# Four 64x64 products that stood in 128-row pairs are put beside the four mixing products, in one section of the step

## The chip, the cores and the metric

The kernel runs on one core of a Trainium2 chip. The metric is the device time of one execution in microseconds; of the kernel before there are three runs, and their median counts. A profile of one further execution is at hand.

## The reference

The input `x` is 16 images of 64 channels and 128 x 128 pixels in float32. Four residual layers follow one another, each on a group norm (32 groups of two channels) of its input:

```
x = x + L0(gn(x))   # gram = xf xf^T / N;  conv_w @ (gram @ xf): a 64x64 mixing of the channels of each image
x = x + L1(gn(x))   # |scharr_x| + |scharr_y|, each channel by itself
x = x + L2(gn(x))   # a quarter of the channels shifted left, a quarter right; 3x3 conv 64->64; bias
x = x + L3(gn(x))   # 3x3 conv 64->64, 1x1 conv 64->64, batch norm over all images, leaky relu, clip to 0..255
```

Layer 3's batch norm needs sums over all images, so the kernel keeps its result in memory and ends with a pass that reads it and layer 3's input back, combines them and writes the output.

## The kernel before, in words

**Tiling.** The 128 partitions hold two halves of 64 channels. For layer 0 and 1 these are the upper and the lower half of an image, eight rows of each at a time (`R = 8`, so an image has `NS = 8` pieces). Layers 2 and 3 hold even and odd rows ("planes"); a piece makes two output tiles of four row pairs.

**Steps and stages.** One loop goes over steps; a step has four quarters, q = 0 to 3. In every quarter the stages run in the order `Layer3`, `Layer2`, `Front` (layers 0 and 1), each on the piece of the image that is due, and then the `Gram` part for a later image. Each image is eight steps behind the one before it, so in a middle step all stages are at work on different images. `InOrder` keeps every engine's instructions in the order in which the program issues them, so each engine is a fixed list; what an instruction waits for on other engines comes from the tiles it touches.

**What TensorE does in a step.** Each layer of 2 and 3 needs per step the shared products (`shared`, into the tile `one`: six products) and two sets of own products (`own`, n = 0 and n = 1, into the two banks of the tile `two`). All of these have 128 rows and 64 columns: the output is the lower 64 partitions or the upper 64, and `issue` alternates them, so that two run side by side in the two column halves of the array. I call two such products side by side a pair slot. `own` works on a difference tile (`diffs`, `d` in the profile: odd rows minus even rows and the like). In one output half both input planes have weights: three products, one for each tap kx. In the other half (`o` from `single`) only one input plane has weights: two of its taps are packed into one product of 128 rows (weights `pk`, source `qd`, a copy of the difference whose second half is shifted by a column), and the last tap, kx = 2, is a product of 128 rows of whose weights 64 rows are zero:

```
some[o] = [
    (p[cols(o), 0:m], pk, q[:, :, 1:1 + W]),
    (p[cols(o), 0:m, 0:W - 1], wt[:, n, 2, cols(o)], d[:, :, 2:1 + W]),
]
```

I call this product the sparse last tap. There are two in each layer and step (n = 0, 1), four in a step.

**The mixing.** For image 3 and later (`four`), the layer-0 product of a piece is four products of 64 rows and 64 columns, in quarter 1 (`mix_four`). `load` puts the first four rows of both image halves into partitions 0 to 63 and the second four into 64 to 127. So the two products of g = 0 use the upper row half of the array and write both column halves of the tile `po`, and those of g = 1 the lower row half and a tile of the pool `ps_g` (`po` too in the profile). The steps with this mixing are 104: 13 images by 8. In them layers 2 and 3 are always at work.

**The order around the change.**
- Quarter 0: VectorE drains layer 2's `two` of the step before (`two<-two,edges`, then `x<-two,c`) and makes layer 2's difference n = 0 (`difference("d2", 0, ...)`); a DMA on GpSimd's queue makes its shifted copy (`twin(0)`, `qd<-d`). TensorE does layer 3's `shared` and `own` n = 0.
- Quarter 1: layer 3's `own` n = 1; `issue_rest` sends what is held back; then `mix_four`; then, in three of eight steps while there are images left, 42 to 44 Gram products (`bank<-xw`).
- Quarter 2: layer 2's `shared`, its tile `two` is taken from the pool (`ps_two`, two buffers, which layers 2 and 3 take in turn), `own` n = 1. ScalarE empties `one` (`c<-one,co`). VectorE drains layer 3's `two` (`y<-two,c`) and makes layer 3's differences (`d3`).
- Quarter 3: layer 2's `own` n = 0, and after it VectorE's difference n = 1 for the next step ("last of 3").

VectorE also does layer 1 (the tiles `u` and `e`), ScalarE the norms, absolute values and sums of squares (`junk`). When an image's layer 2 is through, VectorE reduces its sums (`s<-st`) and makes the next image's weights (`wi`).

Of the kernel before, what the change touches and what calls it, by code (L numbers as in the profile page):

```python
# [16 lines left out]
P = 128  # L17
# [3 lines left out]
R = 8  # L21
# [88 lines left out]
def tile_kernel(ctx: ExitStack, tc: tile.TileContext, x, cw_h, w2_t, b2, wbin_t, w1_t, b1, gamma, beta, consts, out):  # L110
# [56 lines left out]
    def cols(o):  # L167
        return slice(o * C, (o + 1) * C)
# [372 lines left out]
    class Front:  # L541
# [14 lines left out]
        def load(self, i):  # L556
            b = self.b
            t = xin.tile([P, R, W], F32, tag="x", name=f"x_{b}_{i}")
            if self.four:

                t = t.rearrange("p (h r) w -> p h r w", h=2)
                v = x[b].rearrange("c (h r) w -> c h (r w)", h=2)
                for g in range(2):
                    j = (i * R + g * CP) * W
                    sp.dma_start(t[cols(g)].rearrange("p h r w -> p h (r w)"), v[:, :, j:j + CP * W])
            else:
                for h in range(2):
                    sp.dma_start(flat(t[h * C:(h + 1) * C]), halves(x[b].rearrange("c h w -> (c h w)"), h, i * R, R))
            self.xs[i] = t

        def mix_four(self, i):

            for g, (pool, tag) in enumerate(((ps_po, "po"), (ps_g, "g"))):
                self.po[i, g] = pool.tile([P, CP, W], F32, tag=tag, name=f"po_{self.b}_{i}_{g}")
            t = self.xs.pop(i)
            order = 1 - last[0], last[0]
            for g in range(2):
                for h in order:
                    pe.matmul(self.po[i, g][cols(h)], self.abd[cols(g), cols(g)], t[cols(g), h], start=True, stop=True)

        def mix(self, i, g):
            if self.b == 0 and (i, g) in ((0, 1), (1, 0)):
# [15 lines left out]
        def at(self, i, q):  # L598
            b = self.b
            if q == 0:  # L600
                if i == -3:

                    self.xe = xin.tile([P, W], F32, tag="xe", name=f"xe_{b}", bufs=1)
                    sp.dma_start(self.xe[lo], x[b][:, HH, :])
                    sp.dma_start(self.xe[hi], x[b][:, HH - 1, :])
                    sp.dma_start(x2_d[b][0:W].rearrange("(p w) -> p w", p=1), w0[0:1, 0:W])
                if i + 3 < NS and i + 3 not in self.xs:
                    self.load(i + 3)
                if -1 <= i < NS - 1:
                    self.prepare(i + 1, 1)  # L610
                if 1 <= i:
                    self.store(i - 1)
                    act.activation(
                        junk.rearrange("p (j w) -> p j w", w=W), self.x2.pop(i - 1), AF.Square,
                        accum_out=self.st[:, 1, i - 1:i],
                    )
                if i == NS:
                    chains.append(coefficients(self.st, lambda co: coefs2.update({b: co}), b2_sb))
            if q == 1 and -2 <= i < NS - 2:
                if i == -2:  # L620
                    self.abd, self.co = lead.pop(b)
                if i == -2 and not self.four:
                    self.pe = ps_g.tile([P, CP, W], F32, tag="g", name=f"pe_{b}")[:, 0, :]
                    small_product(self.pe, self.abd, self.xe)
                if self.four:
                    self.mix_four(i + 2)
                else:
                    self.mix(i + 2, 0)
            if q == 3 and i == -2 and self.four:
                self.pe = ps_po.tile([P, CP, W], F32, tag="po", name=f"pe_{b}")[:, 0, :]  # L630
                small_product(self.pe, self.abd, self.xe)
            if (i, q) == ((-1, 0) if self.four else (-2, 2)):
                nc.gpsimd.memset(self.chunk(0)[lo, 0, :], 0.0)
                self.normalized(self.chunk(0)[hi, 0, 1:1 + W], self.pe[hi], hi)
                self.pel = small.tile([P, W], F32, tag="pel", name=f"pel_{b}", bufs=1)
                self.normalized(self.pel[lo], self.pe[lo], lo)
            if q == 2:
                if i == NS - 2:
                    nc.gpsimd.memset(self.chunk(NS - 1)[hi, R + 1, :], 0.0)
                    act.copy(self.chunk(NS - 1)[lo, R + 1, 1:1 + W], self.pel[lo])  # L640
            if 0 <= i < NS:
                self.sobel(i, q)
            if q == 2 and -2 <= i < NS - 2:
                self.prepare(i + 2, 0)
            if q == 3 and -2 <= i < NS - 2 and not self.four:
                self.mix(i + 2, 1)
                self.xs.pop(i + 2)
# [71 lines left out]
        pe.matmul(dst, wt, src, start=start, stop=stop)  # L719
        last[0] = o  # L720

    def issue(halves):


        for o in range(2):
            for n, (dst, wt, src) in enumerate(halves[o]):
                held[o].append((dst, wt, src, n == 0, n + 1 == len(halves[o])))
        while held[0] and held[1]:
            o = 1 - last[0]
            emit(o)  # L730
            emit(1 - o)
# [10 lines left out]
    def shared(p, wt, t, m=CP):  # L742
        products(p[:, 0:m], [wt], [by_parity(t)[1][:, 0:m]])

    def own(p, n, table, wt, name, m=CP, both=None):
        d, q, pk = diffs[name][:, n, 0:m], twins[name][:, n, 0:m], packed[f"pk{name[1]}"][:, n]
        o, _ = single(table, n)
        some = [None, None]
        some[1 - o] = taps(1 - o, p[:, 0:m], [wt[:, n] if both is None else both], [d], 1)
        some[o] = [  # L750
            (p[cols(o), 0:m], pk, q[:, :, 1:1 + W]),
            (p[cols(o), 0:m, 0:W - 1], wt[:, n, 2, cols(o)], d[:, :, 2:1 + W]),
        ]
        issue(some)


    tiles3 = {}

    class Layer2:
# [65 lines left out]
        def at(self, i, q):  # L825
# [22 lines left out]
            if q == 1:  # L848
                if i == 0:

                    self.wi = stp.tile([P, 2, 3, P], F32, tag="wi", name=f"wi_{b}", bufs=1)
                    for n, base in ((0, w2[:, 2]), (1, wm)):
                        dve.scalar_tensor_tensor(
                            self.wi[:, n].rearrange("p k o -> p (k o)"), k("I3"), self.co[:, 2:3],
                            base.rearrange("p k o -> p (k o)"), op0=ALU.mult, op1=ALU.add,
                        )
                if -1 <= i < NS - 1:
                    if i == -1:
                        self.co = coefs2.pop(b)
                    t, f = self.v[i + 1], self.whole.pop(i + 1)  # L860
                    act.activation(f, f, AF.Identity, bias=self.co[:, 1:2], scale=self.co[:, 0:1])


                    e = stp.tile([P, 2, R], F32, tag="edges", name=f"edges_{b}_{i + 1}", bufs=3)
                    for side, at in ((0, 0), (1, W + 1)):
                        for rows, j in ((lo, 1), (hi, 0)):
                            n = at + j * W
                            pool.tensor_scalar_mul(
                                e[rows, side], f[rows, n:n + (R - 1) * W + 1:W], self.co[rows, 3 + side:4 + side]
                            )  # L870
                    self.edges[i + 1] = e

                    pool.tensor_scalar_mul(t[:, :, 0], t[:, :, 0], k("keep0"))
                    pool.tensor_scalar_mul(t[:, :, W - 1], t[:, :, W - 1], k("keep1"))
                if i + 2 < NS:
                    self.load(i + 2)
            if q == 2:
                if 0 <= i < NS:
                    t = self.v[i]
                    one = ps_one.tile([P, CP, W], F32, tag="one", name=f"one2_{b}_{i}")  # L880
                    two = ps_two.tile([P, 2, CP, W], F32, tag="two", name=f"two2_{b}_{i}")
                    self.p[i] = two, one
                    shared(one, self.wi[:, 0], t, m)
                    if closing:
                        small_product(one[:, m, :], w0, t[:, R, :])

                    both = self.wi[:, 1]
                    own(two[:, 1], 1, TO_SLOTS, w2, "d2", m, both)
                    if closing:

                        p = two[:, 1, m:CP]
# [8 lines left out]
            if q == 3:  # L900
                if 0 <= i < NS:
                    t = self.v.pop(i)
                    two, one = self.p[i]
                    both = self.wi[:, 1]
                    own(two[:, 0], 0, TO_SLOTS, w2, "d2", m, both)
                    if closing:
                        p, srcs = two[:, 0, m:CP], [t[:, R - 2:R - 1, :], t[:, R - 1:R, :]]
                        issue([taps(0, p, [w2[:, 0], both], srcs), taps(1, p, [both, w2[:, 1]], srcs)])
# [7 lines left out]
    class Layer3:  # L916
# [34 lines left out]
        def at(self, i, q):  # L951
# [10 lines left out]
            if q == 1:  # L962
                if 0 <= i < NS:
                    two, one = self.p[i]
                    own(two[:, 1], 1, TO_PAIRS, w3, "d3")
                    self.v.pop(i)
                    self.c = ring.tile([P, CP * W], F32, tag="c3", name=f"c3_{b}_{i}", bufs=1)
                    act.activation(self.c, flat(one), AF.Identity, bias=b1_sb)
# [82 lines left out]
    for step in range(starts[2][1] - 2, steps):  # L1051
        now[0] = step
        for q in range(4):
# [5 lines left out]
            for stage, at in starts:  # L1059
                if stage is Front and q in (1, 3):  # L1060
                    issue_rest()
                for b in range(B):
                    run(stage, b, step - at - NS * b, q)
            if q in (0, 3):
                for b in range(B):
                    run(Layer2, b, step - starts[1][1] - NS * b, f"last of {q}")
# [116 lines left out]
```

## Time and profile before

| | |
|---|---|
| median of 3 runs | 2716.55 us (2714.24 to 2718.3) |
| the profiled execution | 2713.5 us, of which 2711.7 us are its span |
| PE (TensorE matmul) busy | 2146.4 us (79%) |
| DVE (VectorE) busy | 2116.7 us (78%) |
| ACT (ScalarE) busy | 2069.4 us (76%) |
| POOL (GpSimd) busy | 1042.6 us (38%) |
| stretch with HBM at 420 GB/s, at the end | from about 2230 us to 2711.7 us |

Busy shares are averages over the whole span, so they mix three stages: the start, the steps, and the last pass. The mixing of 64-row products runs from 357.5 us on; the profile starts the steps that are looked at here at each `po<-x,abd 64*64`. In the trace each float32 product is two matmul records of half the time, so that a set of four products counts x8. The column "idle before" names what ended the idle time; "issue" is a wait that the profile can't name.

### The profile page before, as it was taken

How to read it: one execution, taken by the hardware profiler on the slowest of the kernel's cores; microseconds unless marked ns; L12 is line 12 of the kernel's file. 1: busy time of each engine (PE TensorE's matmuls, PEld its weight loads, DVE VectorE, ACT ScalarE, POOL GpSimd, SP SyncE). 2: the span in 40 equal slices, each digit the busy share in tenths (PEclk: the TensorE clock that was granted, in tenths of full speed). 3: DMA queues.
4: the chain of work that ended last, by engine and by line, in shares of the span. 5: the costliest groups of instructions: out<-in, count | busy, mean ns of one | idle time of the engine just before them, and what ended most of it. 6: DMA issues, size and time to landing. Idle time of an engine off the chain costs nothing. (4 is left out here: it accounts for less than half of the span.)

```text
span 2711.7 us, 45518 instructions
## 1 busy us (share of the span) xinstructions
PE 2146.4 (79%) x14804; PEld 905.4 (33%) x14804; DVE 2116.7 (78%) x3111; ACT 2069.4 (76%) x3001; POOL 1042.6 (38%) x1558
## 2 busy tenths in 40 slices
PE   6578899999999999999999999999999992000000
PEld 4234433434343434343434343333335641000000
DVE  4998899898989898989898999999994335333332
ACT  4766889898989898989899989999996666333332
POOL 2266545444445454444445454655554300000000
PEclk8689999999999999999999999999999996555555
DMA  8799889998999889898989888888887879999999
GB/s 208 204 236 241 223 197 245 225 237 222 236 225 241 227 230 230 227 231 232 229 228 237 214 216 204 212 216 218 220 204 187 219 197 327 420 420 420 420 420 374
DMA packets 693596, 685.92 MB, mean 253 GB/s; under 512 B 60096, under 2 KB 580448, under 8 KB 693360
## 3 DMA queue, kind: packets, MB, share of 16 engines
q1 hardware_dynamic: 668208, 613.83, 79.0%
q0 software_dynamic: 25152, 69.18, 10.0%
q8 instruction: 119, 1.95, 0.3%
q14 instruction: 117, 0.96, 0.1%
HBM read 346.23 MB, written 268.44 MB: 227 GB/s over the span
## 5 line engine op out<-in xcount | busy, mean ns | idle before, releaser
L73 PE MATMUL two<-d,w 128*64 128x508 f32 (+2 forms) x2560 | 835.7, 586 | 0.0
L73 PE MATMUL two<-d,wi 128*64 128x508 f32 (+3 forms) x1536 | 571.7, 576 | 0.0
L73 PE MATMUL two<-qd,pk 128*64 128x512 f32 (+1 forms) x1024 | 517.4, 586 | 25.7 <-DMA qd<-d 25.3
L73 POOL DMA_DIRECT2D qd<-d x512 | 272.3, 534 | 686.5 <-DVE d L73 277.9
L73 POOL TENSOR_SCALAR edges<-v,co 64x8 f32<-64x8 f32 x512 | 328.7, 642 | 274.7 <-ACT v L73 195.1
L73 DVE TENSOR_TENSOR d<-v 128x512 f32<-128x512 f32 (+1 forms) x512 | 346.7, 680 | 86.0 <-issue 50.4
L73 PEld LDWEIGHTS two<-d,w 128*64 128x64 f32 x2560 | 272.4, 136 | 322.8 <-issue 282.7
L73 PE MATMUL one<-v,w 128*64 128x508 f32 (+2 forms) x1600 | 364.4, 579 | 1.1 <-ACT v L73 1.1
L73 PE MATMUL one<-v,wi 128*64 128x508 f32 (+3 forms) x1536 | 355.8, 595 | 0.4 <-DVE wi L73 0.3
L73 ACT COPY qd<-d 64x512 f32<-64x512 f32 x512 | 315.6, 616 | 23.3 <-DVE d L73 13.8
L73 DVE SCALAR_TENSOR_TENSOR e<-e 128x1032 f32<-128x1032 f32 (+1 forms) x256 | 313.3, 1224 | 0.0
L73 ACT ACTIVATE xh<-po,co 128x128 f32<-128x128 f32 (+1 forms) x480 | 275.5, 624 | 28.9 <-PE po L73 25.0
L73 PEld LDWEIGHTS two<-d,wi 128*64 128x64 f32 x1536 | 178.6, 135 | 201.3 <-issue 183.2
L73 POOL TENSOR_SCALAR v<-v,kc 128x9 f32<-128x9 f32 x256 | 229.9, 912 | 12.0
L73 DVE SCALAR_TENSOR_TENSOR y<-two,c 128x1024 f32<-128x1024 f32 x128 | 156.0, 1219 | 98.0 <-ACT v L73 45.5
L73 PE MATMUL po<-x,abd 64*64 64x512 f32 (+1 forms) x1024 | 176.6, 639 | 43.9 <-ACT xh L73 38.2
L73 ACT ACTIVATE v<-x,co 128x1024 f32<-128x1024 f32 (+3 forms) x256 | 203.9, 847 | 0.0
L73 ACT ACTIVATE u<-u 128x1024 f32<-128x1024 f32 x128 | 135.6, 1060 | 81.6 <-DVE u L73 80.1
L73 ACT ACTIVATE c<-one,co 128x512 f32<-128x512 f32 x128 | 87.0, 679 | 140.2 <-PE one L73 140.1
L73 PEld LDWEIGHTS two<-qd,pk 128*64 128x64 f32 x1024 | 135.2, 136 | 164.6 <-issue 104.8
L73 PEld LDWEIGHTS one<-v,w 128*64 128x64 f32 x1600 | 130.5, 136 | 175.9 <-issue 147.3
L73 DVE SCALAR_TENSOR_TENSOR u<-xh 128x1170 f32<-128x1170 f32 x128 | 175.5, 1371 | 5.6 <-ACT xh L73 4.5
(160 smaller groups left out, 3432.1 us busy)
## 6 DMA issues: line engine op xcount, KB each, us to landing
x<-in_x SPq DMA_DIRECT2D x256, 256.0 KB, 4.7
x_d<-u SPq DMA_DIRECT2D x512, 128.0 KB, 4.1
y_d<-y SPq DMA_DIRECT2D x512, 128.0 KB, 3.5
x_d<-x SPq DMA_DIRECT2D x496, 128.0 KB, 3.1
xr<-in_x SPq DMA_DIRECT2D x120, 512.0 KB, 6.0
qd<-d POOLq DMA_DIRECT2D x256, 130.0 KB, 3.2
qd<-d POOLq DMA_DIRECT2D x256, 129.8 KB, 3.8
v<-x_d SPq DMA_DIRECT2D x448, 72.1 KB, 2.8
```

Of the source, the lines that this page charges most:

```text
L73: return self.tc.keep_in_program_order(call(*args, **kwargs))
```

## The change

The last taps leave `own` in all steps with mixing. They become products of 64 rows and 64 columns (only the plane that has weights), and go beside the mixing products:

- Layer 3's are noted at q = 1 after its `own` n = 1, and close their sums. Layer 2's are noted at q = 1 too, before its other products of q = 2 and q = 3, and open their sums (`start`); the tile `two` of layer 2 is taken at q = 1 for it.
- `mix_four` is now called for g = 0 and g = 1 and notes its two products each. `load` puts the two image halves into the two partition halves, as for the first three images, so a DMA's runs are 4 KB long where they were 2 KB. The two products of one g then use different row halves and different column halves of the array, and write one bank in different partitions.
- At the end of the quarter `issue_beside` sends layer 3's two taps, the two products of g = 0, layer 2's two taps, and the two products of g = 1.
- Steps without mixing issue what they issued.

On the other four engines the lists of instructions and their waits are the same, but for the shape of those loads. On TensorE the number of products stays the same.

```diff
         def load(self, i):
...
-            if self.four:
-                t = t.rearrange("p (h r) w -> p h r w", h=2)
-                v = x[b].rearrange("c (h r) w -> c h (r w)", h=2)
-                for g in range(2):
-                    j = (i * R + g * CP) * W
-                    sp.dma_start(t[cols(g)].rearrange("p h r w -> p h (r w)"), v[:, :, j:j + CP * W])
-            else:
-                for h in range(2):
-                    sp.dma_start(flat(t[h * C:(h + 1) * C]), halves(x[b].rearrange("c h w -> (c h w)"), h, i * R, R))
+            for h in range(2):
+                sp.dma_start(flat(t[h * C:(h + 1) * C]), halves(x[b].rearrange("c h w -> (c h w)"), h, i * R, R))
...
-        def mix_four(self, i):
-            for g, (pool, tag) in enumerate(((ps_po, "po"), (ps_g, "g"))):
-                self.po[i, g] = pool.tile([P, CP, W], F32, tag=tag, name=f"po_{self.b}_{i}_{g}")
-            t = self.xs.pop(i)
-            order = 1 - last[0], last[0]
-            for g in range(2):
-                for h in order:
-                    pe.matmul(self.po[i, g][cols(h)], self.abd[cols(g), cols(g)], t[cols(g), h], start=True, stop=True)
+        def mix_four(self, i, g):
+            pool, tag = ((ps_po, "po"), (ps_g, "g"))[g]
+            po = pool.tile([P, CP, W], F32, tag=tag, name=f"po_{self.b}_{i}_{g}")
+            t = self.xs[i][:, g * CP:(g + 1) * CP, :]
+            for h in range(2):
+                beside.append((po[cols(h)], self.abd[cols(h), cols(h)], t[cols(h)], True, True))
+            self.po[i, g] = po
...
+    def mixing():
+        i = now[0] - starts[2][1] - NS * EARLY
+        return -2 <= i < NS * (B - EARLY) - 2
+
+    def issue_beside():
+        for n in range(0, len(beside), 2):
+            for dst, wt, src, start, stop in sparse[n:n + 2] + beside[n:n + 2]:
+                pe.matmul(dst, wt, src, start=start, stop=stop)
...
     def own(p, n, table, wt, name, m=CP, both=None, apart=None):
...
+        some[o] = [(p[cols(o), 0:m], pk, q[:, :, 1:1 + W])]
+        if not mixing():
+            some[o].append((p[cols(o), 0:m, 0:W - 1], wt[:, n, 2, cols(o)], d[:, :, 2:1 + W]))
+            issue(some)
+        else:
+            issue(some, *((o, None) if apart == "before" else (None, o)))
+
+    def last_taps(two, table, wt, name, m=CP, first=False):
+        if mixing():
+            for n in range(2):
+                o, i = single(table, n)
+                sparse.append((
+                    two[cols(o), n, 0:m], wt[cols(i), n, 2, cols(o)], diffs[name][cols(i), n, 0:m, 2:2 + W],
+                    first, not first,
+                ))
...
# Layer2.at, q == 1
+                if 0 <= i < NS:
+                    self.two = ps_two.tile([P, 2, CP, W], F32, tag="two", name=f"two2_{b}_{i}")
+                    last_taps(self.two, TO_SLOTS, w2, "d2", m, True)
# Layer2.at, q == 2 and q == 3
-                    own(two[:, 1], 1, TO_SLOTS, w2, "d2", m, both)
+                    own(two[:, 1], 1, TO_SLOTS, w2, "d2", m, both, "before")
# Layer3.at, q == 1
                     own(two[:, 1], 1, TO_PAIRS, w3, "d3")
+                    last_taps(two, TO_PAIRS, w3, "d3")
# the loop over the quarters, after the stages
+            issue_beside()
```

More of the change, by code (lines that the diff above doesn't have):

```diff
@@ L625, in at @@
                 if self.four:
-                    self.mix_four(i + 2)
+                    for g in range(2):
+                        self.mix_four(i + 2, g)
+                    self.xs.pop(i + 2)
                 else:
@@ L720, in emit, with issue @@
         last[0] = o
-    def issue(halves):
+    sparse, beside = [], []
+    def mixing():
[5 more added lines that the diff above has]
+                pe.matmul(dst, wt, src, start=start, stop=stop)
+        for dst, wt, src, start, stop in sparse[len(beside):]:
+            pe.matmul(dst, wt, src, start=start, stop=stop)
+        last[0] = 1
+        sparse.clear()
+        beside.clear()
+    def issue(halves, before=None, after=None):
         for o in range(2):
             for n, (dst, wt, src) in enumerate(halves[o]):
-                held[o].append((dst, wt, src, n == 0, n + 1 == len(halves[o])))
+                held[o].append((dst, wt, src, n == 0 and before != o, n + 1 == len(halves[o]) and after != o))
         while held[0] and held[1]:
@@ L743, in shared, with own @@
         products(p[:, 0:m], [wt], [by_parity(t)[1][:, 0:m]])
-    def own(p, n, table, wt, name, m=CP, both=None):
+    def own(p, n, table, wt, name, m=CP, both=None, apart=None):
         d, q, pk = diffs[name][:, n, 0:m], twins[name][:, n, 0:m], packed[f"pk{name[1]}"][:, n]
@@ L749, in own @@
         some[1 - o] = taps(1 - o, p[:, 0:m], [wt[:, n] if both is None else both], [d], 1)
[L750 to L754, printed above, removed]
+        some[o] = [(p[cols(o), 0:m], pk, q[:, :, 1:1 + W])]
[12 more added lines that the diff above has]
+                ))
     tiles3 = {}
@@ L880, in at @@
                     one = ps_one.tile([P, CP, W], F32, tag="one", name=f"one2_{b}_{i}")
-                    two = ps_two.tile([P, 2, CP, W], F32, tag="two", name=f"two2_{b}_{i}")
+                    two = self.two
                     self.p[i] = two, one
@@ L904, in at @@
                     both = self.wi[:, 1]
-                    own(two[:, 0], 0, TO_SLOTS, w2, "d2", m, both)
+                    own(two[:, 0], 0, TO_SLOTS, w2, "d2", m, both, "before")
                     if closing:
```

## The prediction

> **What bounds the kernel now.** I read the page's 40 slices first, for the stages.
>
> ```profile
> PE   6578899999999999999999999999999992000000
> DVE  4998899898989898989898999999994335333332
> ACT  4766889898989898989899989999996666333332
> ```
>
> A slice is 67.8 us. PE is full from slice 6 to 33, but DVE and ACT stand at 8 to 9 until slice 30 (2006 us): three engines share this stage. Then PE alone is full, to about 2200 us, and the rest is the last pass, where the chain of waits is DMA out, x3 and y in turn. So I cut the stage at each mixing product and took every engine's busy time by windows, one step each. One image is eight steps:
>
> ```profile
> core 0: us, PE busy (x) PEld busy (x) DVE busy (x) ACT busy (x) POOL busy (x), PEclk, DMA share, GB/s
> 1267.79:1285.82 18.03, 18.03 (x170) 8.15 (x168) 17.77 (x30) 15.85 (x26) 7.90 (x13) 1.00 0.90 222
> 1285.82:1303.79 17.97, 17.97 (x174) 7.92 (x172) 16.26 (x27) 14.34 (x22) 5.63 (x10) 1.00 0.73 179
> 1303.79:1321.62 17.83, 17.83 (x170) 7.58 (x168) 15.44 (x28) 13.40 (x22) 11.49 (x18) 1.00 0.99 253
> 1321.62:1337.21 15.59, 15.59 (x115) 9.29 (x113) 11.42 (x19) 15.46 (x24) 7.52 (x12) 1.00 1.00 260
> 1337.21:1352.17 14.96, 14.96 (x77) 4.80 (x76) 14.85 (x24) 13.95 (x22) 8.02 (x10) 1.00 0.95 237
> 1352.17:1368.68 16.51, 15.07 (x74) 5.08 (x73) 16.48 (x22) 16.19 (x26) 8.24 (x12) 1.00 0.93 261
> ...
> sum 130.83, PE 129.39 PEld 52.41 DVE 121.80 ACT 118.95 POOL 62.17; mean PE 16.17 PEld 6.55 DVE 15.22 ACT 14.87 POOL 7.77
> ```
>
> The reader is to see that PE's 129.39 of 130.83 us hides a change of bound. In the first three steps PE also does Gram products and DVE has air. In the fourth ACT has none (15.46 of 15.59). From the fifth on DVE has none, and in the sixth PE itself idles 1.44 us. The timelines of the engines give the joints:
>
> ```profile
> 1295.06 0.69 DVE L73 TENSOR_TENSOR d<-v 128x512 f32<-128x512 f32 x1 [1.52 <-issue]
> 1310.53 0.69 ACT L73 ACTIVATE c<-one,co 128x512 f32<-128x512 f32 x1 [4.33 <-PE one L73]
> 1337.05 0.17 DVE L73 TENSOR_REDUCE s<-st 128x2 f32<-128x16 f32 x1 [3.43 <-ACT junk L73]
> ```
>
> DVE waits at 1295.06 until PE has read the difference it overwrites; ACT waits at 1310.53 for PE's `one`; then ACT runs gapless to 1337 and DVE waits for it; then DVE runs with no gap over 0.25 us to its first wait on PE at 1276.99 in the picture of one image earlier, that is 1407.8. So an image's 130.8 us are a ring: DVE 70.8, PE 33.5 (1276.99 to 1310.53), ACT 26.5. **Only what PE saves in its third of the ring counts.**
>
> **What the Trainium skill says.** "TensorEngine Tiling (Array Packing)", Key Properties: tiles run independently, and a change of tiling mode drains the array. The trace agrees, with its prices:
>
> ```profile
> 1302.84 1.02 PE L73 MATMUL two<-d,w 128*64 128x508 f32 x4
> 1303.79 1.09 PE L73 MATMUL po<-x,abd 64*64 64x512 f32 x8
> 1304.81 0.28 PE L73 MATMUL bank<-xw 128*64 128x65 f32 x2
> ```
>
> The four mixing products (x8) take 1.02 us to the next start. A pair slot takes 0.853 us (`two<-d,wi` at 1355.82 to the same place of the next tap at 1356.68 is 0.86). Four tiles thus cost one pair slot plus 0.16 of drain. The same page, Gotcha 1, says that different row tiles can't use the same PSUM bank at once; "PSUM — Partial Sum Buffer", PSUM bank collisions raise a hardware error, narrows this to one bank and 32-partition quadrant. The trace of before doesn't show the case: there the two row halves write different banks. After, the two products of a g write one bank from different row halves, in different quadrants. The second page would let them overlap, and so do I; the first is a rival below.
>
> **The change part by part.**
>
> *TensorE, per step.* Removed: four sparse taps, that is two pair slots, 2 x 0.853 = 1.71 us. Mixing grows from one set of four to two: 1.02 becomes 2 x 0.853 + 0.16 = 1.87. Net 0.853 us a step, 88.7 us over 104 steps. That is work, not time. The new section is unseen: bounds 1.87 (all overlap) and 3.57 (nothing across row halves, 4 x 0.853 + 0.16); I take 1.87. No cheaper end is to be had: 16 records in four tiles are 1.71 alone.
>
> *The new wait.* Layer 2's taps stand in the middle of the section and need `x<-two,c` done (the bank is free) and the difference n = 0, DVE's next instruction. Before, PE needed this difference only in quarter 3. Behind the wait on PE stand the products of g = 1, Gram, and `one`, and for these ACT. In the PE third the price is nil: the difference is done at 1282.0 and 1300.1, the sections start at 1285.82 and 1303.79, over 3.6 us later, and layer 2's taps come 0.85 us into them. In the DVE stretch PE arrives early and will wait here; DVE doesn't care: `one` follows 0.85 + 2.6 us after the difference and ACT's `c` in a light step comes about 5.7 after it. That the shifted copy is needed later in PE's list (one pair slot less before it, one set more) leaves the wait `two<-qd,pk` (1.44 us at 1359.99) off the path too.
>
> *Layer 3's sum* closes in the first set, 1.02 us after the section's start instead of 0.17. `y<-two,c` came 1.6 us after that start or later (1287.43 against 1285.82), and PE's lead covers the rest: nothing. The POOL and SP queues keep order and waits. The loads' 4 KB runs move the same bytes; PE waited for `x` once, 5.7 us: nothing.
>
> *What an image gains.* (a) Head start: at the section of 1267.79 the difference is there at 1266.5. PE, 0.85 us faster in each of the steps before, can be in the section's second half then, so start at 1265.7, 2.1 earlier; the section is 0.85 longer: 1.25 net. (b) Two further full steps to `one` at 1310.53: 2 x 0.853 = 1.71. Together 2.96 us; DVE's own waits on PE in this third (0.20 + 1.52 + 2.25 = 3.97) leave room for it. Then ACT, and so DVE's `s`, come 2.96 earlier. Late next is DVE, everywhere else in the ring.
>
> *Sum.* Nine such images (sections from 480 to 1613 us): 9 x 2.96 = 26.6. The steps from 357 to 480: DVE waits 1.84 us at one `s`, with ACT waiting more than that on PE before it: 1.8. The 26 steps after 1613 without Gram products: DVE is busy 205.16 of 210.10 us in the last 14; what PE can give back there are the waits at two `s` (1.18 and 1.96, ACT having waited for `one` before both): 3.1. At the end PE leaves the mixing 0.85 us ahead of the difference instead of 2.57 behind (1900.72 against 1898.15), and to 2200 us PE alone bounds: 3.4. The last pass is DMA's and only starts earlier. Total **34.9 us**. The profiled execution took 2713.5 (span 2711.7 and 1.8 around it), so 2678.6; it lies 3.05 below the median of 2716.55, so **2682** against that.
>
> **The rivals.**
>
> *PE is the bound in each step*, as its full row of nines says: the whole 88.7 us come, 2628. For it: PE has no gaps. Against: DVE's 14.85 of 14.96 and 16.48 of 16.51. A part of it (PE's lead carried over image borders) would give 2640 to 2660.
>
> *Slower: row halves that share a bank don't overlap.* The section costs up to 3.57. The point from which it decides is 1.02 + 1.71 = 2.73 us; above it PE gets slower than before, and PE has only 1.44 us of air per image. At 3.57 a step gains 0.85: an image's PE work becomes 129.4 + 6.8 = 136.2, 5.4 over now, nine times 49; of the other 33 or so steps nearly all are PE-full, 0.75 each, 25: 2790. For it: the page's sentence, and that no such set is in the trace. Against: pairs of `two<-d` share a bank from two column halves and overlap fully.
>
> *Nothing shows.* The ring's ACT and DVE parts stretch by what PE gives (ACT is within 0.13 us of full in the fourth step, and one `xh<-po` a little later would do): within 5 us of 2716.
>
> **How the numbers follow.** Central case 0.66 (2660 to 2708), whole or larger gain 0.10, nothing 0.06, slower 0.18 (most of it the shared bank, the rest a wait in the section that I priced at nil). A measurement of this kernel tells about 0.2%, 5.4 us, from no change. Faster 0.76, same 0.06, slower 0.18. The range 2640 to 2722 leaves out some 0.05 below and 0.13 above. The likeliest case's own range is 2660 to 2708.
>
> **What would show it.** In the profile after: `two<-d,w 64*64` and `po<-x,abd 64*64` in one section of 1.8 to 1.9 us where PE doesn't wait; DVE idle per image down from 9.0 to about 6 us; steps in the DVE stretch as long as now (14.4 to 16.5) with PE idle showing up in them; ACT's 4.33 us before `c<-one` about halved; the Gram steps 17.1 to 17.3 us instead of 18; the last pass as long as before. Wrong: sections of 2.7 us or more; or steps of 14.0 us in the DVE stretch (then DVE was not the bound); or DVE waits on `two` that were not there.

## The result, and the profile after

The kernel after took 2684.64 us (median of 4 runs, 2683.2 to 2690.18), the kernel before 2716.45 us (4 runs, 2714.24 to 2718.3). The ratio is 0.9887 with a 95% interval of 0.987 to 0.9904: 31.8 us faster, where 34.9 were worked out. The profiled execution of after is the slowest of its four, 2690.18 us with a span of 2688.4; against before's profiled 2713.5 it shows only 23.3 us, and the stages below add up to that number.

The page's slices of the kernel after:

```profile
PE   6578899999999999999999999999999992000000
DVE  4999899899999899999999999999994325333332
ACT  4766889898989898989899989999986676333332
```

PE's row of nines is what it was, although PE does less (a nine stands for anything from 90% up). The windows between the starts of the mixing sections, the same image as before (span; then busy time and instructions of PE, PEld, DVE, ACT, POOL; granted clock, DMA share, GB/s):

```profile
1254.61:1271.81 17.20, 17.20 (x172) 7.63 (x170) 17.10 (x31) 15.84 (x26) 8.57 (x14) 1.00 0.90 224
1271.81:1288.94 17.13, 17.13 (x176) 7.62 (x174) 16.69 (x28) 14.46 (x24) 6.04 (x10) 1.00 0.77 189
1288.94:1305.90 16.96, 16.96 (x172) 7.42 (x170) 15.45 (x28) 13.41 (x20) 9.88 (x17) 1.00 1.05 255
1305.90:1321.28 15.38, 15.38 (x117) 8.01 (x115) 13.04 (x18) 15.28 (x24) 8.49 (x12) 1.00 0.99 258
1321.28:1337.27 15.99, 14.80 (x80) 4.83 (x79) 14.13 (x22) 14.95 (x25) 8.64 (x12) 1.00 0.91 240
1337.27:1353.72 16.45, 14.45 (x76) 4.71 (x75) 16.38 (x23) 16.18 (x25) 7.89 (x11) 1.00 0.94 247
```

The three Gram steps lost 0.83 to 0.87 us each. The three steps after them together take 47.82 us where they took 47.06, and PE now idles in two of them (15.99 against 14.80, 16.45 against 14.45). One of the new sections, from PE's timeline:

```profile
1271.81 0.65 PE L73 MATMUL po<-x,abd 64*64 64x512 f32 x2
1272.28 0.59 PE L73 MATMUL two<-d,w 64*64 64x512 f32 x2
1272.29 0.60 PE L73 MATMUL po<-x,abd 64*64 64x512 f32 x2
1272.71 0.59 PE L73 MATMUL two<-d,w 64*64 64x512 f32 x2
1272.72 0.60 PE L73 MATMUL po<-x,abd 64*64 64x512 f32 x2
1273.14 0.60 PE L73 MATMUL two<-d,w 64*64 64x512 f32 x2
1273.15 0.59 PE L73 MATMUL po<-x,abd 64*64 64x512 f32 x2
1273.68 1.54 PE L73 MATMUL bank<-xw 128*64 128x65 f32 x41
```

From 1271.81 to 1273.68 it is 1.87 us, the sum of two pair slots and the drain. (The section has 16 records. The first two, layer 3's `two` at 1271.80, have the same names as the products before them, so the view counts them to the row above, which isn't shown.) So the two row halves that write one bank in different partitions do overlap: of the two pages of the Trainium skill that the prediction set against each other, the measurement sides with the narrower rule in "PSUM — Partial Sum Buffer" (one bank and quadrant) and not with Gotcha 1 of "TensorEngine Tiling (Array Packing)".

The joints of the ring, from the timelines of ACT and DVE:

```profile
1296.49 0.69 ACT L73 ACTIVATE c<-one,co 128x512 f32<-128x512 f32 x1 [3.45 <-PE one L73]
1299.09 0.56 DVE L73 TENSOR_TENSOR d<-v 128x384 f32<-128x384 f32 x1 [1.37 <-POOL co L73]
1323.07 0.17 DVE L73 TENSOR_REDUCE s<-st 128x2 f32<-128x16 f32 x1 [2.74 <-ACT junk L73]
```

DVE's waits in PE's third fell from 3.97 us to 1.62 (0.25 at 1281.90 and the 1.37 here), ACT's wait for `one` from 4.33 to 3.45. (The profile puts the 1.37 down to `co` on POOL, but that was done at 1298.12. PE's last products that read the overwritten difference end at about 1299.0, by modelled ends, which is when DVE starts: the wait is still one for PE.) One image, from one `s<-st` to the next (1323.07 to 1451.41), takes 128.34 us with DVE busy 121.71; before (1337.05 to 1467.97) 130.92 with 121.72.

### The profile page after: what moved, and what is told of

It is laid out like the page before. It is cut to its first block, busy times and chain, and to the rows that moved or that the text cites. A ratio compares the mean times of both kernels' runs of the same rounds, so it can differ in the third digit from the quotient of the medians.

```text
span 2688.4 us, 45530 instructions
## 1 busy us (share of the span) xinstructions
PE 2095.1 (78%) x14804; PEld 867.8 (32%) x14804; DVE 2116.6 (79%) x3111; ACT 2070.9 (77%) x3001; POOL 1044.5 (39%) x1558
## 5 line engine op out<-in xcount | busy, mean ns | idle before, releaser
L73 PE MATMUL two<-d,w 128*64 128x508 f32 (+3 forms) x2560 | 747.7, 593 | 17.3 <-DVE d L73 17.2
L73 PE MATMUL two<-d,wi 128*64 128x508 f32 (+3 forms) x1536 | 496.3, 579 | 0.0
L73 PEld LDWEIGHTS two<-d,w 128*64 128x64 f32 (+1 forms) x2560 | 229.2, 135 | 383.4 <-issue 353.3
L73 ACT COPY qd<-d 64x512 f32<-64x512 f32 x512 | 315.5, 616 | 23.3 <-DVE d L73 13.8
L73 PE MATMUL po<-x,abd 64*64 64x512 f32 (+1 forms) x1024 | 271.3, 637 | 45.3 <-ACT xh L73 42.6
L73 PEld LDWEIGHTS two<-d,wi 128*64 128x64 f32 x1536 | 156.9, 136 | 189.2 <-issue 179.5
L73 PEld LDWEIGHTS one<-v,w 128*64 128x64 f32 x1600 | 124.2, 136 | 188.2 <-issue 154.3
L73 ACT ACTIVATE v<-v,co 128x1154 f32<-128x1154 f32 x128 | 172.2, 1345 | 16.4 <-DMA v<-x_d 16.4
```

Of the source, the lines that this page charges most:

```text
L73: return self.tc.keep_in_program_order(call(*args, **kwargs))
```

## The experiments

To compare kernels by stage I take two stretches between the `s<-st` that open an image's layers, in each profiled execution: nine images with Gram products (the fifth `s<-st` to the 23rd; before 418.61 to 1596.52), and from there to the last `s<-st` (2182.51), mostly without. Each ratio is against runs of before that were taken beside it. A profiled execution lies up to 5.5 us from its kernel's median. The last column repeats well (582.3, 582.5 and 582.4 in after, e1 and e3, which run the same products); in the column before it a few us can be chance.

| kernel | median us | ratio to before (95%) | nine Gram images | then to the last `s` |
|---|---|---|---|---|
| before | | | 1177.9 | 586.0 |
| after | 2684.64 | 0.9887 (0.987 to 0.9904) | 1158.2 | 582.3 |
| e1_after_again | 2687.93 | 0.9898 (0.9881 to 0.9914) | 1159.2 | 582.5 |
| e2_pad | 2719.2 | 1.0017 (1.0008 to 1.0025) | 1181.7 | 587.5 |
| e3_order | 2689.47 | 0.9909 (0.9894 to 0.9924) | 1161.2 | 582.4 |
| e4_pool_diff | 2710.02 | 0.9977 (0.997 to 0.9984) | 1166.9 | 594.2 |
| e5_pad2 | 2793.79 | 1.0288 (1.0271 to 1.0305) | 1228.7 | 610.9 |
| e6_lite_before | 2694.68 | 0.9923 (0.9908 to 0.9937) | 1170.6 | 584.8 |
| e7_lite_after | 2654.06 | 0.9773 (0.9754 to 0.9793) | 1149.0 | 567.4 |
| e8_early_square | 2686.72 | 0.989 (0.9871 to 0.9908) | 1153.5 | 586.9 |
| e9_lite_act | 2677.95 | 0.9861 (0.9846 to 0.9875) | 1148.8 | 580.2 |
| e10_lite_both_after | 2647.37 | 0.9737 (0.9709 to 0.9764) | 1151.7 | 565.2 |
| e11_lite_both_before | 2687.15 | 0.9893 (0.9878 to 0.9908) | 1164.3 | 584.9 |
| e12_lite_both_dma | 2613.2 | 0.962 (0.9607 to 0.9633) | 1117.2 | 565.4 |

### Is it TensorE's work? (e1, e2, e3, e5)

e1 is the kernel after, once more. e2 gives back the saved 0.853 us a step by issuing the two products of g = 0 twice, and leaves all else of the change. e5 issues all four twice; e3 sends the four taps ahead of the four mixing products.

```diff
# e2_pad
-            for dst, wt, src, start, stop in sparse[n:n + 2] + beside[n:n + 2]:
+            for dst, wt, src, start, stop in sparse[n:n + 2] + beside[n:n + 2] + (beside[0:2] if n == 0 else []):
# e5_pad2
+            for dst, wt, src, start, stop in sparse[n:n + 2] + beside[n:n + 2] + beside[n:n + 2]:
# e3_order
-        for n in range(0, len(beside), 2):
-            for dst, wt, src, start, stop in sparse[n:n + 2] + beside[n:n + 2]:
...
+        for dst, wt, src, start, stop in sparse + beside:
```

> The changed kernel once more, unedited. Ring theory (an image's time is a DVE part, a PE part and an ACT part in turn, and only the PE part got shorter): 2683 to 2686 us, images in the Gram stage of 128.3 us. The first profile also has ACT waiting 16.4 us for layer 2's loads (v<-x_d), 3.2 before. If that belongs to the change, because the same bytes move in less time, the second profile shows ten or so such waits again; if it is chance, it shows about two and a span 5 to 7 us shorter.

> The two mixing products of g = 0 are issued twice in the section (same values), which gives TensorE back 0.853 us a step and leaves order, waits and loads as in the changed kernel. Section 2.72 us instead of 1.87. Ring theory: TensorE's part of an image is as long as before the change, so 2711 to 2722. If the gain came from the loads' longer runs or from the order alone: 2685. If TensorE were the bound in every step of the changed kernel: 2684.6 + 104 x 0.853 = 2773.

> Same products, other order: all four last taps first, then all four mixing products. The first four use two tiles of the array, the last four the other two. If products start in the order of the list, each four take 1.71 us and the section 3.57, 0.85 more per step than before the change: TensorE's work in an image is 136.2 us and sets the pace, 2770 to 2795. If TensorE lets later products on free tiles pass earlier ones: section 1.87 and 2685.

> All four mixing products are issued twice in the section: 1.71 us more than in the changed kernel, section 3.57, the price of the prediction's slower rival. Ring theory: the first 0.853 us only filled TensorE's air (2719 in the single repetition, 0.33 us a step); the second is nearly all time, because TensorE's work in an image goes from 130.5 to 137.3 us against 132.3 measured: 5 x 9 images, 0.85 x 26 steps after them, some more at the start: 2785 to 2800. If each repetition costs the same: 2754.

e2 came out at 2719.2 us, 0.17% above before: with the work given back the whole gain is gone, so it is TensorE's work and neither the longer DMA runs nor the new order of products. e1 repeats the gain (27.5 us against the median of before beside it, 2715.45). e3 shows that the order inside a section is worth little: 0.9909 against 0.9898, intervals that overlap.

e5 shows something more. From e2 to e5 another 0.853 us a step was added, and it cost 74.6 us, where the same 0.853 between after and e2 was worth about 33 (2719.2 less 2686.3, the middle of after and e1). In e5 PE has no wait at all in the nine images, and the section is 3.58 us throughout. So **the kernel before stood on a knee**, a point where the price of TensorE's work changes: above it the work counts more than four fifths of itself (74.6 of 88.7), below it little over a third. e5 also bears out the price in the prediction's slower rival, whose cause did not come true: at a section of 3.57 that was 2790, and here, by other means, it is 2793.79.

### What stops the gain below the knee? DVE, as predicted? (e6, e7, e4, e8)

e6 and e7 take one VectorE instruction out of layer 1's piece (`u<-u`, 1.14 us from its start to the next one's; DVE's busy time falls by 0.97 us a piece) in the kernels before and after; the horizontal difference of that piece isn't computed.

```diff
-                dve.tensor_sub(gx, h[:, :, 2:W + 2], gx)
```

> The kernel before, with one of layer 1's eight VectorE instructions left out (u<-u, the horizontal difference; 1.14 us from start to next start, once a step), so its output is not the reference's. Ring theory: TensorE has only 1.4 us of air in an image, so little of 8 x 1.14 us comes through: 2700 to 2712. If VectorE alone sets the pace: 128 x 1.14 = 146 us less, 2570.

> The changed kernel with the same VectorE instruction left out. Ring theory: TensorE's air of 3.6 us in an image (124.75 busy of 128.34) is used up: 9 x 3.4 and 3 x 2: 2643 to 2655. So the change is worth some 55 us where VectorE has air, against 32 with it. If the 32 us were all that the change takes off TensorE's path: 32 below the other light kernel, 2670 to 2680.

The change is now worth 40.6 us (2694.68 to 2654.06), not the 55 or so expected, and e6's own gain is larger than expected because 10.7 us of it lie ahead of the fifth `s<-st` (418.61 against 407.89), in the start, which the expectation had left out. By stage it splits clearly. After the Gram images the change was worth 3.7 us (586.0 to 582.3) and becomes 17.4 (584.8 to 567.4): there DVE was the bound below the knee, as predicted. In the nine Gram images it was worth 19.7 and becomes 21.6. **There DVE alone is not what stopped the gain.**

e4 tried to relieve DVE without dropping work: layer 2's difference n = 1 goes to GpSimd. e8 removes the joint at `s<-st` by squaring an image's last layer-2 piece a quarter earlier on ScalarE.

```diff
# e4_pool_diff
-                difference("d2", 1, self.v[i + 1], CP if i + 2 < NS else CP - 1)
+                difference("d2", 1, self.v[i + 1], CP if i + 2 < NS else CP - 1, pool)
# e8_early_square
# Layer2.at, q == 0, after x<-two,c
+                if i == NS:
+                    self.square(i - 1)
...
-            if q == "last of 0" and i == NS:
-                self.square(i - 1)
```

> The changed kernel with layer 2's difference n = 1 (d<-v, 0.60 us from start to next start on DVE, once a step) made by GpSimd, which is 39% busy and also sends the copy that follows. Ring theory: DVE's parts get shorter: about 5.5 x 0.6 = 3.3 us in an image with Gram products (nine), about 4 in one without (three): 2640 to 2655. Rival: GpSimd takes 2 us or more for it or slows DVE down, the shifted copy comes late and TensorE waits for it: 2685 to 2720.

> The changed kernel with the sum of squares of an image's last layer-2 piece (ACT, junk<-x) moved ahead of two ACT instructions, right behind x<-two,c, so that DVE's s<-st waits less. Ring theory: the joint from ACT to DVE comes 2.1 us earlier in the nine images with Gram products (s at 1320.95 instead of 1323.07 in the profile) and 0.9 in the two after: 20 us, 2662 to 2669. If DVE's wait there is made good elsewhere (TensorE or ScalarE being the bound in the image as a whole): 2680 to 2686.

e4 lost most of the gain: 2710.02, in the rival's range. Two pairs of instructions from one image of e4 show why, each on its own engine but overlapping in time:

```profile
1352.79 2.13 POOL L73 TENSOR_TENSOR d<-v 128x512 f32<-128x512 f32 x1
1353.72 2.44 DVE L73 SCALAR_TENSOR_TENSOR u<-xh 128x1170 f32<-128x1170 f32 x1
1369.81 1.23 DVE L73 TENSOR_TENSOR e<-xh 128x1040 f32<-128x1040 f32 x1
1370.09 2.10 POOL L73 TENSOR_TENSOR d<-v 128x512 f32<-128x512 f32 x1
```

and the means of these groups in one image of the kernel after (line, engine, operation, shapes, count | busy, mean ns | idle before):

```profile
L73 DVE TENSOR_TENSOR d<-v 128x512 f32<-128x512 f32 x30 | 20.6, 687 | 0.4 <-POOL v L73 0.2 <-issue 0.2
L73 DVE SCALAR_TENSOR_TENSOR u<-xh 128x1170 f32<-128x1170 f32 x8 | 11.0, 1370 | 0.8 <-DMA x_d<-u 0.8
L73 DVE TENSOR_TENSOR e<-xh 128x1040 f32<-128x1040 f32 x8 | 9.9, 1234 | 0.0
```

The moved instruction takes 0.69 us on DVE. On GpSimd it takes 1.27 us where it starts first or alone, and up to 2.13. Which of the two engines pays depends on which started first. In the first pair GpSimd did: `u<-xh` took 2.44 us, 1.07 more than its usual 1.37, and GpSimd's instruction was still running for the first 1.20 us of it. In the second pair DVE did: it kept its 1.23 us and GpSimd took 2.10. In this image five DVE instructions that started behind a GpSimd difference grew by 4.9 us in all, and the differences moved away had taken 5.4. So DVE has eight instructions less an image and is as busy as ever: 121.87 us against 121.71. The Trainium skill's "SBUF — State Buffer", Who interferes with whom, states that a VectorE instruction with two SBUF inputs contends with a GpSimd instruction that reads SBUF. Here both are of that kind, and the trace agrees.

e8 missed the 2662 to 2669 of the ring theory and lies at the edge of its alternative (2680 to 2686). DVE's wait at `s<-st` fell to 0.67 us in most images (it had been 1.2 to 3.5), and the nine images came 4.7 us sooner (1158.2 to 1153.5), but the rest took 4.6 us more (582.3 to 586.9), and the median stayed. Shortening this joint of the ring brought nothing by itself.

### ScalarE, or both, or the loads? (e9, e10, e11, e12)

In the light steps ACT is about as full as DVE (14.95 of 15.99 and 16.18 of 16.45 us in the windows, DVE 14.13 and 16.38). e9 takes out one of its instructions, e10 takes out that and DVE's, and e11 is the kernel before without both.

```diff
# e9_lite_act
-                act.activation(gy, gy, AF.Abs)
# e10_lite_both_after, e11_lite_both_before
-                act.activation(gy, gy, AF.Abs)
-                dve.tensor_sub(gx, h[:, :, 2:W + 2], gx)
```

> The kernel after without the second ACTIVATE e<-e (Abs) of layer 1's piece: one ACT instruction of about 1.06 us less in each of 80 steps with a piece (84.8 us of ACT work in all); the rest of the computation goes on with the values not made absolute. DVE's and PE's work is as in the kernel after. Theory 'DVE and ACT are both full in the steps without a Gram': relieving ACT alone brings about 0.5 to 1 us an image and a few us in the start ramp: 2668 to 2684. Rival 'ACT alone sets that part of an image': five of eight steps lose 1.06 us, 3 to 4 us an image over 9 images and as much in the steps without Gram: 2635 to 2660. Rival 'DVE alone': 2684 to 2692, as the kernel after.

> The kernel after without two instructions of layer 1's piece: VectorE's tensor_sub u<-u (0.9 us) and ScalarE's second Abs e<-e (1.06 us), so that both engines are lighter and PE is left as the bound; those parts of the piece are not computed. Theory 'DVE and ACT are both full': an image falls from 128.3 to PE's own 124.8 us or below (PE's busy time also held stretched products), 2610 to 2640. Rival 'DVE alone was full': as without u<-u alone, 2648 to 2660.

> The kernel before without the same two instructions. With DVE and ACT both lighter PE sets nearly every step, and the section's 0.853 us a step (88.7 us over 104 steps) should show almost whole between this kernel and the changed one without the two: a difference of 60 to 85 us, so about 2685 to 2700 here. If DVE alone was the other bound the difference stays at the 40 us seen without u<-u alone, and this kernel takes 2692 to 2697.

e9 lay in the range of "both are full", but e10 missed it: 2647.37 where 2610 to 2640 was expected, and between e11 and e10 the change is worth 39.8 us, not 60 to 85. The theory of two full engines does not hold. The totals lie about where the rival "DVE alone was full" had them (2648 to 2660, and 40 us), but neither engine holds up the nine Gram images: TensorE idles 35.3 us in them in the kernel after, 30.2 in e7, 27.8 in e9 and 32.8 in e10. Lightening one or both hardly shortens these waits. (By the table relieving DVE brought 9.2 us there, ACT 9.4, both together 6.5. That both bring less than one isn't shown: e10's four runs spread from 2638.08 to 2653.24, and its profiled one is 5.1 us above the median, e7's 3.5 below.)

The windows of the nine Gram images say more. Of e11 (before, both lighter):

```profile
403.07:1567.33 1164.26, 1161.81 (x8242) 469.16 (x8240) 1020.57 (x1566) 998.19 (x1537) 553.27 (x853) 1.00 0.93 233
```

and of e10 (after, both lighter):

```profile
404.00:1555.73 1151.73, 1118.89 (x8247) 442.44 (x8244) 1020.47 (x1567) 1000.86 (x1537) 547.54 (x855) 1.00 0.93 234
```

e11 is bound by PE alone: 1161.81 of 1164.26 us busy. In e10 no engine is full: PE idles 32.8 us, DVE 131. The DMA share is 0.93 in both, so the share by itself tells nothing; but in e10 the waits of those images (total us, times, longest) name loads and stores that are late:

```profile
ACT v L73 <- DMA v<-x_d: 42.1, 28, 4.6
DVE u L73 <- DMA x_d<-u: 24.9, 22, 2.8
```

In e11 these two are 8.4 and 9.1 us, and TensorE, busy throughout, does not wait for what follows from them.

So the last run leaves most of the Gram's row loads out of e10: three chunks are loaded once and copied again for the later images, whose Grams are then of the wrong rows.

```diff
         def load(self, m):
-            t = xin.tile([P, C // 8, W], F32, tag="xr", name=f"xr_{self.b}_{m}", bufs=3)
-            sp.dma_start(t, x[self.b].rearrange("c h w -> h c w")[:, m * C // 8:(m + 1) * C // 8, :])
-            self.xr[m] = t
+            if m % 3 not in kept:
+                t = xin.tile([P, C // 8, W], F32, tag="xr", name=f"xr_{self.b}_{m}", bufs=3)
+                sp.dma_start(t, x[self.b].rearrange("c h w -> h c w")[:, m * C // 8:(m + 1) * C // 8, :])
+                kept[m % 3] = t
+            self.xr[m] = kept[m % 3]
```

> The kernel after without the two instructions of the piece (u<-u on VectorE, the second e<-e on ScalarE) and, besides, without most of the Gram's row loads: xr<-in_x (512 KB each, 8 an image, 4.2 of the 30 MB that an image moves) is issued for three chunks only, and the later images copy those three tiles again, so their Grams are of the wrong rows. Nothing else moves. Theory 'the DMA engines are the next limit' (in the run without the two instructions they were busy 92 to 94% of an image, 102% in its last three steps, and v<-x_d came up to 5.8 us late): the DMA share falls to about 0.81, the waits for v<-x_d and x_d<-u go, images come every 124 to 126 us instead of a mean of 128, and the whole falls by 18 to 35 us, to 2612 to 2630. Rival 'the stops of TensorE in steps without a Gram (two<-d for DVE, two<-qd for its copy) are what is left': loads are no limit, the waits go but the images stay at 127 to 128: 2640 to 2650.

2613.2 us, in the range of the load theory and far from its rival's. The five runs lie within 3.5 us, where e10's four spread over 15. The nine Gram images of e12:

```profile
399.94:1517.10 1117.16, 1106.88 (x8240) 436.58 (x8234) 1017.82 (x1566) 997.19 (x1537) 557.68 (x853) 1.00 0.84 209
```

The DMA share fell to 0.84, PE's idle time to 10.3 us, the waits for `v<-x_d` and for the store `x_d<-u` are gone from ACT and DVE, and the images came evenly, every 124.4 to 124.9 us in the middle of the stage, where e10 had 125.8 to 130.1. The issues with their KB and median us to landing show that layer 2's loads come sooner. In e10:

```profile
v<-x_d SPq DMA_DIRECT2D x252, 72.1 KB, 3.4
v<-x_d SPq DMA_DIRECT2D x126, 144.2 KB, 3.7
```

and in e12:

```profile
v<-x_d SPq DMA_DIRECT2D x252, 72.1 KB, 2.8
v<-x_d SPq DMA_DIRECT2D x126, 144.2 KB, 2.6
```

(In e11 they took 3.1 and 3.8 us: as long as in e10, but TensorE's own work was longer.) Against e11 the change is now worth 74 us (2.73% of before, from the ratios 0.9893 and 0.962). The kernel before without these loads wasn't run, but e11 had only 2.5 us of PE idle in the nine images, so lighter loads could have brought it hardly more there; and 74 is what the same 0.853 us cost above the knee from e2 to e5.

**What stays open:** e12 takes away the transfers and with them 8 entries an image in SP's list. Whether layer 2's loads came late because the DMA engines were full or because they stood behind the row loads on the queue isn't told apart. (SP's queue itself waited 16.9 us, in 20 waits, for a row load to land in e10's nine images, and 11.0 us in e11's. That fits the second and doesn't settle it.) The row loads weren't taken out of the kernel after itself, so their share of its missing 57 us, with DVE and ACT as they are, isn't known either.

## Why the prediction was right, point by point

**The bound.** The windows' reading, that PE's 129.4 of 130.8 us is not the whole bound, held. But the two stood closer than "only PE's third counts" sounds. PE without any wait takes 129.2 us an image (e11), 1.7 below the ring. Both limits were met at once, and that is the knee.

**The section** of 1.87 us held where PE doesn't wait in it, and with it the rejection of the slower rival. The Gram steps (17.20, 17.13, 16.96), DVE's idle time (128.34 - 121.71 = 6.6 us an image, about 6 predicted), PE idling in the light steps, and the last pass (529.2 us from the last `s<-st` to the end before, 529.4 after) are as forecast. One sign was not: ACT's 4.33 us before `c<-one` was to halve and became 3.45.

**The new wait** was there, once an image, in the section of the first light step:

```profile
1339.60 0.65 PE L73 MATMUL two<-d,w 64*64 64x512 f32 x2 [1.26 <-DVE d L73]
```

Priced at nil, and rightly so here: DVE has no gap around it. It turns up in the bill once the rest is gone: in e12, whose images PE bounds, it is 1.12 us of an image's 124.42.

**The terms of the sum**, by the profiled executions (how much earlier each `s<-st` came):

| term | predicted | measured |
|---|---|---|
| 357 to 480 us | 1.8 | about 0 |
| nine Gram images | 26.6 | 19.8 |
| steps without Gram | 3.1 | 2.1 |
| lead at the end | 3.4 | 1.6 |
| total | 34.9 | 23.5 at the last `s<-st`, 23.3 in the execution |

The medians differ by 31.8 because this execution of after is 5.5 us above its own median and that of before 3 below. So 8.5 of the apparent shortfall of 11.6 are the two executions, and 3.1 the sum's own. e1's profiled execution gives much the same terms (-0.6, 18.7, 2.0 and 1.5), but it too is 4.1 us above its median; and by medians e1 gained 27.5, so the sum is 3 to 7 us too high. The term that was over-sized is the Gram image. 2.96 was predicted. The first eight images of before take 130.3 to 132.1 us each, five of after's 128.2 to 128.4; the image followed above gained 2.6. Two whole steps came as said (0.85 each), the head start came to about 0.8 instead of 1.25: the difference was ready at 1254.88, 0.6 us before the tap that reads it, so it was not the difference that PE had to wait for. DVE waits 2.35 us less in PE's third and 0.69 less at `s<-st`, and part of that was spent again in between: 0.66 us before `u<-xh`, for the store `x_d<-u` of the tile that it overwrites. In the nine images this wait grew from once, 0.5 us, to seven times, 6.1 us. Two images gained less still or lost (131.6 us against 130.3 before, and 130.6 against 131.9) with late loads, `v<-x_d`, in them; the waits between 460 and 560 us:

```profile
ACT v L73 <- DMA v<-x_d: 5.1, 3, 2.2
```

Before's Gram images have no such wait. The first of the two is as long in e1 (131.6), the other isn't (128.3). These two images stand 5.6 us above the usual 128.3, about the 5.5 by which this execution exceeds its median; whether the faster executions lack such images isn't shown.

**"Late next is DVE, everywhere else in the ring"** is the sentence that didn't hold. It is true of the steps without Gram (e7). In the Gram images relieving DVE, ACT or both gives back about 1 us an image and leaves TensorE idle for 28 to 33 us of the nine, and only with the row loads gone as well come another 34.5 us (1151.7 to 1117.2; by the medians of e10 and e12 34.2). The prediction had weighed only the loads of `x`, whose bytes don't change, and put them at "nothing"; on layer 2's loads and the row loads it has no term. At the old pace they cost nothing (e11 has no PE idle to show for them). At the new pace, with DVE and ACT lighter, they cost 34 us; in the kernel after as it stands DVE, ACT and the loads are all candidates, and their shares are open.

## What to carry to other kernels

An engine's saved time is worth its full price only while that engine is the only one late. Ask how far the next limit is, and test it on both sides: the same 0.853 us a step was worth 33 us below the starting point and 75 above, and two padded kernels show that. When relieving one engine brings little, and relieving two leaves the first one idle as before, look for a resource that all of them share; here, with DVE and ACT lighter, it was the row loads, which no engine's busy row shows. And look at single instructions before trusting a mean: e4's `u<-xh` has a mean of 1.72 us, made of 1.37 and of 2.05 to 2.44.

## What the runs showed of the hardware that was not expected

- Products on tiles that are free start beside products listed before them. In e3 the four taps are listed ahead of the mixing, and yet PE's timeline has both from the start, `po` 0.02 us behind each pair of `two`:

```profile
1273.45 0.59 PE L73 MATMUL two<-d,w 64*64 64x512 f32 x2
1273.47 0.59 PE L73 MATMUL po<-x,abd 64*64 64x512 f32 x2
1273.88 0.59 PE L73 MATMUL two<-d,w 64*64 64x512 f32 x2
1273.90 0.60 PE L73 MATMUL po<-x,abd 64*64 64x512 f32 x2
```

  The first pair of each kind started at 1272.97 and 1272.99. From its first record the section took 1.89 us where nothing in it had to wait, 1.88 in the order of the change. But where layer 2's taps had to wait for DVE nothing passed them: the mixing products listed behind started only after them, and such sections took about 4.25 us in e3 against 3.39 in the kernel after. The Trainium skill's "TensorE: Matmul & The Clock Gate", Part 3, states a strict order of matmuls in start and end; in e3 the starts differ from it (the ends are modelled, so they tell nothing here).
- A VectorE and a GpSimd instruction, each with two float32 inputs, ran nearly one after the other when they met (e4). The one that started second grew by almost the whole overlap (`u<-xh` by 1.07 us of 1.20), so that moving one of four differences to GpSimd freed no time on VectorE.
